# A two-layer graph attention kernel: twelve node tiles of source alphas gathered from a DRAM table, and W1's last third run first

## The chip, the core and the metric

The kernel runs on one core of a Trainium2 chip. The metric is the device time of one execution in microseconds (us). Times are compared as medians of several runs.

A core has five engines with queues of their own that matter here. PE multiplies matrices, and loads its weights beside that (PEld). DVE works on vectors, ACT applies activation functions and copies with a scale, and POOL issues the gathers (DMAs whose rows are picked by a list of indices) and a few other DMAs. SP issues most of the plain DMAs. Each works through its queue in order, and semaphores tie them together.

## The reference

A graph has 3125 nodes with 768 features and 53,125 edges, sorted by destination: 25,000 random pairs in both directions, and a loop at each node. The input is normalised and passed through a relu, and two attention layers follow, with residuals.

```python
def gat_conv(x, edge_index, W, a_src, a_dst, bias, heads, out_ch, concat):
    xl = (x @ W).reshape(n, heads, out_ch)
    alpha_src = einsum('nhc,hc->nh', xl, a_src)
    alpha_dst = einsum('nhc,hc->nh', xl, a_dst)
    e = leaky_relu(alpha_src[src] + alpha_dst[dst], 0.2)
    e = exp(e - segment_max(e, dst)[dst])
    alpha = e / (segment_sum(e, dst)[dst] + 1e-16)
    out = segment_sum(xl[src] * alpha[:, :, None], dst)
    ...
h0 = relu(layernorm(x))
h1 = relu(layer_norm(gat_conv(h0, W1, 4 heads of 256))) + h0 @ Wr1 + br1
h2 = layer_norm(gat_conv(h1, W2, 1 head of 768)) + h1 @ Wr2 + br2
return x + h2
```

So each edge needs, for each of the four heads of layer 1, the alpha of its source node and that of its destination node, and the row of its source node.

## The kernel before, in words

The nodes are cut into 25 tiles (NB) of 128, the last of 53. The edges that end in one node tile are laid out as 17 columns (J) of 128 slots. An alpha of an edge is kept in `al1[slot, column, head, node tile]`. The change lies in layer 1, ahead of its weighted sums, where three stages follow one another.

**First stage: products.** `ring` holds eight tiles of x. A loop over b runs from -2 to 25. In each turn DVE takes the statistics of tile b + 2 (`stats`) and normalises tile b + 1 (`normal`, L814), PE transposes tile b and ACT applies the relu (`flip`, L822), and then two things are interleaved by hand. The first is the product of h0 with W1. W1 is extended by eight columns, the weights folded with a_src1 and a_dst1 (`fold`), so that the product also gives the alphas of each node. It has 1032 columns, cut in three thirds of 344 (`product(b, i)`, L854). The last third (i = 2) holds the alphas. They go into `asad1` and `known` counts the tiles that have them. The finished row goes to `table1` in DRAM, from where layer 1 gathers later. `products` (L875) runs all three thirds of a tile, one tile after another, apart from the first three tiles. W1 is loaded by thirds, too.

The second thing is the side work, the generator `beside` (L945), of which `quota` says how many steps a turn takes: one or two in the first turns, then two, and three from turn 13 on. Its steps, in order: the fold of W1 with a_src1 and a_dst1 (four steps), the list of edges (`edge_list`, L253, with the two matmuls of L315 and L358 that sum the edges by node), the first step of `windows` (L363, which starts a gather of the list), the fold of W2 (`fold_w2`, L882), the rest of `windows` (which gives `idx_s`, the source node of each slot, and tables in DRAM of 16-bit lists), and `own_lookups` (L906). The last compares lists with node numbers to find, by bf16 matmuls, the destination's alpha of each slot. It takes the alphas in groups, as `known` allows. The comparison (`one_hot`) is stored in `hot_d` for layer 2 as an 8-bit float, by a converting DMA of POOL (L931), and ACT counts its ones into `cnt` (L934).

The orders of PE, ACT and DVE in this stage are those of the program. After the loop come the products that are left, six steps of `early` (L993: h0 times Wr1 for twelve tiles, 144 matmuls as written), and what is left of the side work. Each matmul in fp32 is two instructions of the profile.

**Second stage: source lookups** (L1075). The alphas of the sources need a lookup over all nodes. For each of 25 node tiles, a list of 2176 low parts of the source numbers is spread over all partitions and compared with the node number (`one_hot`), 51 matmuls pick for each slot the alphas of the 25 nodes with that low part (`source_values`, L553), DVE multiplies these with a mask of the high part, and one reduction writes `al1[:, :, :, b]` (L567). Between the tiles PE takes four or five steps of `early` (112 in all).

**Third stage: softmax** (`weights`, L598). It transposes `al1` (L581), scans along the lists for the largest alpha and applies the exponential, with 26 more steps of `early` between. Then the weighted sums of layer 1 begin (L758), with gathers of 4 KB rows of `table1` by POOL (L197). The first ten of these are issued as soon as `table1` is whole. The layer 2 that follows isn't touched.

## Time and profile before

| what | value |
|---|---|
| runs shown (three) | median 1917.48 us, from 1916.97 to 1924.33 |
| the profiled execution | 1923.87 us; its span 1922.0 us; mean granted clock 0.96 |
| busy: PE, DVE, ACT, POOL | 1759.3, 1000.4, 443.7, 898.9 us |
| W1 products: first and last start | 11.7 to 302.4 us |
| source lookups: first and last start | 313.0 to 476.0 us |
| first weighted sum of layer 1 | 507.0 us |

The page gives one line per group of instructions: line of the code, engine, operation, what is written from what, shapes, count, then the busy time, the mean duration of one in ns, and the idle time of the engine just ahead, with what ended it. A timeline has one line per instruction or run of like instructions: start and duration in us, then the same names; the bracket has the idle time before it and what ended that. Durations of matmuls overlap, so that PE's rate is read from one start to another. A view of windows gives the busy time of each engine in stretches of the span.

### The profile page before, as it was taken

Reading aid. Unit: us, or ns where it says so; the run is one execution under the profiler, and the core shown is the slowest. Engines: PE = TensorE matmul, PEld = TensorE weight load, DVE = VectorE, ACT = ScalarE, POOL = GpSimd, SP = SyncE. Lnnn points to the kernel's source line nnn. Section 1 sums busy time; section 2 is a strip of 40 time slices with the busy share of each in tenths; the row PEclk is TensorE's granted clock in tenths of the full one; section 3 lists DMA queues with packets and bytes.
Section 4 is the critical chain, followed back from the end, with each engine's and each line's share of the span. In section 5 each row is a group of like instructions: output and inputs, shape, how many; then the busy total and the mean of one; then the engine's idle time right before and its main releaser. Section 6 shows DMA issues by size and latency. Waiting matters only on the chain. (4 is left out here: it accounts for less than half of the span.)

```text
span 1922.0 us, 31113 instructions
## 1 busy us (share of the span) xinstructions
PE 1759.3 (92%) x11411; PEld 957.8 (50%) x11411; DVE 1000.4 (52%) x2641; ACT 443.7 (23%) x1286; POOL 898.9 (47%) x922
## 2 busy tenths in 40 slices
PE   8999998999879999999998998969888898988895
PEld 5666664666446655555554554434333333333331
DVE  7673434888845566466466556312433443344345
ACT  2122331000211212112111211212322332333233
POOL 2000102000365666566566666156566666666662
PEclk9999999999889999999998999889889999989998
DMA  7824538331598999999899999488888998988984
GB/s 236 281 96 144 135 110 295 115 126 64 203 407 314 367 372 348 356 374 385 329 356 378 349 377 333 156 324 313 302 286 324 329 328 325 327 311 310 328 284 157
DMA packets 173673, 540.78 MB, mean 281 GB/s; under 512 B 33086, under 2 KB 58452, under 8 KB 173384
## 3 DMA queue, kind: packets, MB, share of 16 engines
q0 software_dynamic: 100912, 381.05, 55.2%
q1 hardware_dynamic: 68206, 147.26, 21.9%
q10 hardware_dynamic: 4394, 10.39, 1.4%
q8 instruction: 93, 1.52, 0.3%
q14 instruction: 68, 0.56, 0.1%
HBM read 498.62 MB, written 65.62 MB: 294 GB/s over the span
## 5 line engine op out<-in xcount | busy, mean ns | idle before, releaser
L197 POOL DMA_INDIRECT g<-table,idx_s x406 | 405.2, 998 | 411.7 <-DVE m L635 179.2
L201 POOL DMA_INDIRECT g<-table,hi_s x426 | 437.7, 1027 | 291.7 <-issue 88.8
L758 PE MATMUL pa<-g,w 128*32 128x256 f32 x3912 | 275.9, 395 | 32.6 <-issue 23.9
L1377 PE MATMUL pa<-g,w 128*32 128x384 f32 x1956 | 248.8, 510 | 58.9 <-issue 54.4
L182 PE MATMUL pr<-wr,h 128*128 128x384 f32 x768 | 288.0, 516 | 3.8 <-issue 3.8
L182 PE MATMUL p<-w,h1T 128*128 128x384 f32 (+1 forms) x768 | 278.7, 511 | 2.2 <-DVE h1T L1181 1.6
L758 PEld LDWEIGHTS pa<-g,w 128*32 128x32 f32 x3912 | 131.7, 112 | 166.3 <-issue 78.7
L182 PEld LDWEIGHTS pr<-wr,h 128*128 128x128 f32 x768 | 144.8, 200 | 126.2 <-issue 58.2
L182 PEld LDWEIGHTS p<-w,h1T 128*128 128x128 f32 x768 | 145.1, 197 | 123.9 <-issue 32.5
L735 DVE TENSOR_TENSOR w<-oh,al 128x128 f32<-128x128 f32 (+1 forms) x416 | 132.0, 317 | 130.5 <-PE pa L758 75.0
L1377 PEld LDWEIGHTS pa<-g,w 128*32 128x32 f32 x1956 | 63.7, 111 | 221.4 <-issue 208.4
L1341 DVE CUSTOM_DVE_ANT_0 e<-mix,pen 128x640 f32<-128x640 f32 x25 | 20.6, 825 | 290.4 <-remote 132.3
L863 PE MATMUL pm<-w,h0l 128*128 128x344 f32 (+1 forms) x468 | 140.8, 455 | 0.0
L182 PE MATMUL pr<-h0k,wr 128*128 128x256 f32 (+1 forms) x576 | 140.1, 390 | 0.0
L1000 PE MATMUL pm<-h0g,wr 128*128 128x512 f32 x288 | 132.7, 607 | 0.1
L863 PE MATMUL pm<-w,h0g 128*128 128x344 f32 x432 | 131.0, 459 | 0.3 <-ACT h0g L842 0.3
L182 PEld LDWEIGHTS pr<-h0k,wr 128*128 128x128 f32 x576 | 106.2, 190 | 29.5 <-issue 9.0
L931 POOL DMA_DIRECT2D hot_d<-ohd x25 | 13.4, 538 | 219.5 <-DVE own L513 120.6
L734 DVE TENSOR_SCALAR oh<-iota_f,rel_s 128x32 f32<-128x32 f32 (+1 forms) x416 | 113.4, 272 | 0.1
L863 PEld LDWEIGHTS pm<-w,h0l 128*128 128x128 f32 (+1 forms) x468 | 84.8, 185 | 44.1 <-issue 5.7
L863 PEld LDWEIGHTS pm<-w,h0g 128*128 128x128 f32 x432 | 81.9, 193 | 40.8 <-issue 1.7
L1320 ACT ACTIVATE slots<-g 128x32 f32<-128x32 f32 x416 | 65.1, 219 | 117.8 <-DMA g<-table,idx_s 77.7
(288 smaller groups left out, 1666.8 us busy)
## 6 DMA issues: line engine op xcount, KB each, us to landing
s<-slo_d SPq DMA_DIRECT2D x25, 544.0 KB
table<-row SPq DMA_DIRECT2D x24, 512.0 KB
own<-table SPq DMA_DIRECT2D x24, 512.0 KB
h1T_d<-h1T SPq DMA_DIRECT2D x24, 512.0 KB
h<-h1T_d SPq DMA_DIRECT2D x22, 512.0 KB
table<-row SPq DMA_DIRECT2D x24, 392.0 KB
ring<-in_x_dram SPq DMA_DIRECT2D x24, 384.0 KB
xr<-in_x_dram SPq DMA_DIRECT2D x24, 384.0 KB
```

Of the source, the lines that this page charges most:

```text
L182: nc.tensor.matmul(out_, lhsT, rhs, start=start, stop=stop)
L197: nc.gpsimd.indirect_dma_start(out=g, out_offset=None, in_=table[:, :], in_offset=bass.IndirectOffsetOnAxis(ap=idx_s[:, c], axis=0))
L201: nc.gpsimd.indirect_dma_start(out=g, out_offset=None, in_=table[:, :], in_offset=bass.IndirectOffsetOnAxis(ap=idx_k[:, c], axis=0), bound ...
L734: nc.vector.tensor_scalar(oh, iota_f[:, lo:hi], rel_s[:, c:c + 1], None, op0=OP.is_equal)
L735: nc.vector.tensor_tensor(w, oh[:, None, :].to_broadcast([128, heads, hi - lo]), al[:, POS[j], :, b:b + 1].to_broadcast([128, heads, hi - ...
L758: nc.tensor.matmul(pa[p0:p0 + 32, o // f, o % f:o % f + n], w[:, o // cols, :], g[:, o:o + n], start=to not in opened, stop=False, skip_gr ...
L863: nc.tensor.matmul(pm[:r, :C], h0[b][:, k, :], w1[:, k, i * C:(i + 1) * C], start=(k == 0), stop=(k == NK1 - 1))
L931: nc.gpsimd.dma_start(hot_d[b], ohs[b])
L1000: nc.tensor.matmul(pm, wr1[:, k, m * 128:(m + 1) * 128], groups[gi][:, k, :], start=(k == 0), stop=(k == NK1 - 1))
L1320: nc.scalar.activation(slots[b % 2][:, POS[j], :], gs[b, j][:, C2:C2 + 1].to_broadcast([128, 32]), AF.Copy)
L1341: nc.vector.tensor_tensor_reduce(out=e, in0=mix[:, :WIN], in1=pen, scale=1.0, scalar=-BIG, op0=OP.add, op1=OP.max, accum_out=top)
L1377: nc.tensor.matmul(pa[p0:p0 + 32, i, :f], w_, g[:, i * f:(i + 1) * f], start=(i, q) not in opened, stop=False, skip_group_check=True)
```

## The change

- Source alphas of tiles 0 to 11 (`gathered`) are no longer looked up. `asad1`'s source half is written, in four pieces, to a new table in DRAM, `as1_d` (16 bytes per node), and the new generator `alphas` has POOL gather it, one DMA for each column of 128 slots, into `got`; POOL copies each finished tile into its column of `al1`.
- So that the alphas of all nodes are there early, the loop over b runs the last third of W1 for every node tile as soon as it is flipped, with one or two products per turn (`turns`). The first two thirds of tiles 3 to 24 (`rest`), but for five products that are put in turns 9 to 13, come after the loop, and there side work and gathers are interleaved with them.
- The row of a tile is stored in two parts, the last third on its own.
- The side work has a new order (the fold of W2 behind all of `windows`, nine empty steps ahead of its second step) and new quotas: three steps in turns 3 to 7, one in 8 to 13, then two.
- The one-hot of the own lookups is converted to 8 bits by ACT, in the instruction that counts, and SP stores it.
- The second stage runs for tiles 12 to 24 (`looked`), with the same 112 steps of `early` spread over 13 tiles.

```diff
--- before.py
+++ after.py
@@ -138,6 +138,7 @@
     keep_d = dram.tile([H * NB, S + 2], BF16, name="keep_d")
     hot_d = dram.tile([NB, 128, WIN], F8, name="hot_d")
     ball_d = dram.tile([C2], F32, name="ball_d")
+    as1_d = dram.tile([NB * 128, H], F32, name="as1_d")
 
     ident = const.tile([128, 128], F32, name="ident")
     make_identity(nc, ident)
@@ -786,6 +787,7 @@
             ring = mp.tile([128, NK1 * HC // D, D], F32, tag="B", name="ring")
             AHEAD = NK1 * HC // D
             h0, groups, later_in = {}, [], {}
+            gathered, looked = range(12), range(12, NB)
             so = right.enter_context(tc.tile_pool(name="so1", bufs=1, side="right"))
             own = so.tile([128, J, 2 * H, NB], F32, name="own")
             tabs = so.tile([P, 3, H, NB], BF16, name="tabs")
@@ -847,37 +849,51 @@
                             nc.sync.dma_start(h0T_d[i][:, :, :cols_of(i)], later_in[i])
 
                 C = W1C // 3
-                LEAD = 3
                 rows1 = {}
                 known = 0
+                saved = [9, 17, 23, NB]
 
                 def product(b, i):
 
                     nonlocal known
                     r = rows_of(b)
                     if i == 0:
-                        rows1[b] = wp.tile([P, HC], F32, name="row", bufs=LEAD)[:r]
-                    row = rows1[b]
+                        rows1[b] = wp.tile([P, 2 * C], F32, name="row", bufs=3)[:r]
+                    row = wp.tile([P, HC - 2 * C], F32, name="rowa", bufs=3)[:r] if i == 2 else rows1[b]
+                    o = 0 if i == 2 else i * C
                     pm = pm1.tile([128, 512], F32, name="pm", bufs=3)
                     for k in range(NK1):
                         nc.tensor.matmul(pm[:r, :C], h0[b][:, k, :], w1[:, k, i * C:(i + 1) * C],
                                          start=(k == 0), stop=(k == NK1 - 1))
                         if k == NK1 - 1:
                             e = min((i + 1) * C, HC) - i * C
-                            nc.scalar.activation(row[:, i * C:i * C + e], pm[:r, :e], AF.Copy)
+                            nc.scalar.activation(row[:, o:o + e], pm[:r, :e], AF.Copy)
                             if e < C:
                                 nc.scalar.activation(asad1[:r, b, :], pm[:r, e:C], AF.Copy)
                                 known = b + 1
-                                store_rows(nc.sync, table1, b, row)
+                                store_rows(nc.sync, table1[:, 2 * C:], b, row)
+                                if known in saved:
+                                    g0 = ([0] + saved)[saved.index(known)]
+                                    nc.sync.dma_start(
+                                        as1_d.rearrange("(b p) v -> p b v", p=128)[:, g0:known, :],
+                                        asad1[:, g0:known, :H])
+                            elif i == 1:
+                                store_rows(nc.sync, table1[:, :2 * C], b, rows1.pop(b))
                         if k % 3 == 2:
                             yield
 
-                def products():
-                    for b, i in ((0, 0), (1, 0), (0, 1), (2, 0), (1, 1), (2, 1), (0, 2), (1, 2), (2, 2)):
+                ahead_of = [(0, 0), (1, 0), (0, 1), (2, 0), (1, 1), (2, 1)]
+                rest = [(b, i) for b in range(3, NB) for i in range(2)]
+                turns = {1: ahead_of[:2], 2: ahead_of[2:4], 3: ahead_of[4:], 4: [(0, 2), (1, 2)],
+                         5: [(2, 2), (3, 2)], 6: [(4, 2), (5, 2)]}
+                for b in range(7, NB + 1):
+                    turns[b] = [(b - 1, 2)]
+                    if 9 <= b < 14:
+                        turns[b].append(rest.pop(0))
+
+                def products(todo):
+                    for b, i in todo:
                         yield from product(b, i)
-                    for b in range(LEAD, NB):
-                        for i in range(3):
-                            yield from product(b, i)
 
                 def fold_w2():
                     with tc.tile_pool(name="wf", bufs=2, side="right", reuse_waits="tile") as fp:
@@ -906,7 +922,6 @@
                 def own_lookups():
 
                     with tc.tile_pool(name="sd1", bufs=1, side="right", reuse_waits="tile") as sb:
-                        junk = sb.tile([128, WIN], BF16, name="junk")
                         ohs, tabd = {}, {}
                         ds_ = {b: window(sb, b) for b in range(3)}
                         yield
@@ -928,10 +943,11 @@
                         for b in range(NB + 1):
                             if b < NB:
                                 ohs[b] = one_hot(sb, ds_.pop(b), WIN, "ohd")
-                                nc.gpsimd.dma_start(hot_d[b], ohs[b])
                                 if b + 3 < NB:
                                     ds_[b + 3] = window(sb, b + 3)
-                                nc.scalar.activation(junk, ohs[b], AF.Copy, accum_out=cnt[:, b:b + 1])
+                                hot = sb.tile([128, WIN], F8, name="hot", bufs=3)
+                                nc.scalar.activation(hot, ohs[b], AF.Copy, accum_out=cnt[:, b:b + 1], saturate=False)
+                                nc.sync.dma_start(hot_d[b], hot)
                             if b in upto:
                                 while known < min(upto[b] + 1, NB):
                                     yield
@@ -939,8 +955,6 @@
                             if b:
                                 own_values(own, b - 1, own_products(H, pp, ohs.pop(b - 1), tabd[b - 1]))
                             yield
-
-                products_ = products()
 
                 def beside():
 
@@ -952,14 +966,15 @@
                         yield from edge_list(ep, pp)
                     lists = windows(pp)
                     next(lists)
-                    yield
-                    yield from fold_w2()
+                    for _ in range(9):
+                        yield
                     for _ in lists:
                         yield
+                    yield from fold_w2()
                     yield from own_lookups()
 
                 work = beside()
-                quota = {-2: 1, -1: 0, 0: 1, 1: 2, 2: 2}
+                quota = {-2: 1, -1: 0, 0: 1, 1: 2, 2: 2, 3: 3, 4: 3, 5: 3, 6: 3, 7: 3}
                 for b in range(2):
                     fetch(b)
                 for b in range(-2, NB + 1):
@@ -980,12 +995,14 @@
                         flip(b)
                     if b <= 3:
                         stats(b + 2)
+                    todo = products(turns.get(b, ()))
                     for i in range(3):
-                        if b > 0:
-                            next(products_, None)
-                            next(products_, None)
-                        if i < quota.get(b, 2 if b < 13 else 3):
+                        for _ in range(2 if b < 7 else 1 if i < 2 else 9):
+                            next(todo, None)
+                        if i < quota.get(b, 1 if b < 14 else 2):
                             next(work, None)
+                    for _ in todo:
+                        pass
                 wr1 = mp.tile([128, NK1, HC], F32, tag="B", name="wr1")
                 for k in range(NK1):
                     nc.sync.dma_start(wr1[:, k, :], Wr1[k * 128:(k + 1) * 128, :])
@@ -1007,9 +1024,32 @@
                                             nc.sync.dma_start(r1T_d[soon[gi * GB + i]][:, m - 1:m + 1, :], rt[:, i])
                                 yield
 
+                def alphas():
+
+                    ready = []
+                    for b in gathered:
+                        got = so.tile([128, J, H], F32, name="got", bufs=3)
+                        for j in range(J):
+                            nc.gpsimd.indirect_dma_start(
+                                out=got[:, POS[j], :], out_offset=None, in_=as1_d[:, :],
+                                in_offset=bass.IndirectOffsetOnAxis(ap=idx_s[:, b * J + j:b * J + j + 1], axis=0))
+                        ready.append((got, b))
+                        if len(ready) > 1:
+                            t, o = ready.pop(0)
+                            nc.gpsimd.tensor_copy(al1[:, :, :, o], t)
+                        yield
+                    t, o = ready.pop(0)
+                    nc.gpsimd.tensor_copy(al1[:, :, :, o], t)
+
                 fill = early()
                 sum_biases(mp)
-                for _ in products_:
+                asks = alphas()
+                for n, _ in enumerate(products(rest)):
+                    if n % 2:
+                        next(work, None)
+                    if n % 6 == 0:
+                        next(asks, None)
+                for _ in asks:
                     pass
                 for _ in range(6):
                     next(fill)
@@ -1072,8 +1112,8 @@
                     by_chunk(g1, None, NK2, g1_c)
                     by_chunk(be1, None, NK2, be1_c)
                     slots = ends_of_lists()
-                    for b in range(NB):
-                        for _ in range(4 + b % 2):
+                    for n, b in enumerate(looked):
+                        for _ in range((n + 1) * 112 // len(looked) - n * 112 // len(looked)):
                             next(fill, None)
                         t = sb.tile([128, S], I16, name="s", bufs=2)
                         nc.sync.dma_start(t, slo16_d[b * S:(b + 1) * S][None, :].to_broadcast([128, S]))
```

## The prediction

> **What bounds the kernel now.** I read the windows first, then PE's and DVE's instructions in order of time in the first stage, then one node tile of the second stage, then POOL. The profiled execution took 1923.87 us, 1.87 us of it outside the span of 1922.0 us; the median of the runs shown is 1917.48 us. I work out a difference against the profiled execution and take it off the median.
>
> ```profile
> 0.00:50.00 50.00, 40.69 (x146) 27.54 (x147) 37.76 (x162) 10.97 (x30) 11.89 (x29) 1.00 0.73 238
> 100.00:150.00 50.00, 50.00 (x202) 33.72 (x201) 38.91 (x68) 10.42 (x30) 0.00 (x0) 1.00 0.32 102
> 200.00:250.00 50.00, 50.00 (x238) 33.71 (x238) 22.87 (x69) 19.57 (x55) 6.91 (x13) 1.00 0.50 139
> 400.00:450.00 50.00, 50.00 (x491) 32.04 (x489) 42.94 (x57) 4.12 (x6) 0.00 (x0) 1.00 0.36 123
> ```
>
> Columns: stretch and length, then busy time and count of PE, PEld, DVE, ACT, POOL, then clock, DMA share, GB/s. PE has no idle time from 100 us on, in the stage of the products (to 302 us) and in that of the source lookups (to 476 us). DVE is nearly full in the lookups and in the first 150 us, where the lists of edges are made. POOL does nothing in 400 to 450. So the change takes work from PE and DVE where both are full, and gives it to an idle engine.
>
> ```profile
> 399.83 1.77 PE L562 MATMUL pq<-tabs,ohs 128*128 128x100 bf16 x36
> 401.45 4.52 PE L1000 MATMUL pm<-h0g,wr 128*128 128x512 f32 x10
> 405.80 2.45 PE L562 MATMUL pq<-tabs,ohs 128*128 128x100 bf16 x51
> 408.09 3.66 PE L1000 MATMUL pm<-h0g,wr 128*128 128x512 f32 x8
> ...
> 476.00 4.52 PE L1000 MATMUL pm<-h0g,wr 128*128 128x512 f32 x10
> ...
> 480.36 2.02 PE L581 MATMUL pq<-ident,al 128*100 128x128 f32 x17
> ```
>
> A node tile's lookups are 51 matmuls in 408.09 - 405.80 = 2.29 us; ten matmuls of the filling product last 405.80 - 401.45 = 4.35 us, 0.435 each (a written fp32 matmul is two of them). The filling is not removed: it has 112 steps in this loop, before and after. At 480.36 al is transposed for the softmax, 4.36 us behind the last lookups: this is the point that everything later hangs on.
>
> **Removed.** Twelve tiles' lookups are 12 x 2.29 = 27.5 us of PE, and DVE loses twelve times its share. Of the 13 tiles that stay, each has 112 / 13 = 8.62 filling steps: 17.2 x 0.435 + 2.29 = 9.79 us of PE. Their DVE work is four products, a one-hot, a mask and a reduction:
>
> ```profile
> L564 DVE TENSOR_TENSOR scr<-pq,ohh 128x500 f32<-128x500 f32 x75 | 49.9, 677 | 27.6 <-PE pq L562 21.7 <-remote 5.9
> L567 DVE TENSOR_REDUCE al<-scr 128x68 f32<-128x1700 f32 x25 | 48.0, 1920 | 0.1
> L530 DVE TENSOR_SCALAR ohs<-s,node_f 128x2176 bf16<-128x2176 int16 x25 | 19.6, 785 | 2.4 <-DMA s<-slo_d 2.4
> L1082 DVE TENSOR_TENSOR ohh<-iota_f,hi_s 128x425 bf16<-128x425 f32 x25 | 14.9, 596 | 1.1 <-DMA ball_d<-ball_v 1.1
> ```
>
> That is about 5.7 us (the fourth product is shorter), so PE alone bounds the stage: 13 x 9.79 = 127.3 us.
>
> From the last product (its start is the 302.4 of the first row below) to the transposes of al: 12 filling matmuls (5.2), the 13 tiles (127.3), 4.4 behind them: 136.9 us. Before, it was 480.36 - 302.4 = 178 us, 13 us more than the sum of its parts (5.2 + 25 x 6.22 + 4.4 = 165), because own lookups and the first one-hots came late there, behind the last product:
>
> ```profile
> L863 PE MATMUL pm<-w,h0l x468: 452/452/557, 17.5 to 302.4; 128*128 128x344 f32 x144, 128*53 128x344 f32 x12
> ...
> 302.80 0.39 PE L545 MATMUL pd<-tabd,ohd 128*128 128x96 bf16 x5
> 303.02 5.38 PE L1000 MATMUL pm<-h0g,wr 128*128 128x512 f32 x12
> ...
> 313.01 2.37 PE L562 MATMUL pq<-tabs,ohs 128*128 128x100 bf16 x46
> ```
>
> After, own lookups end among the products, and 5.2 us and 8.6 filling steps cover the first one-hot. So if the first stage stays as long as it is, the gain is 178 - 136.9 = 41 us.
>
> **Moved: the order of the first stage.** PE's work there is the same, but no longer spread evenly. Until now each node tile brings three products and one flip:
>
> ```profile
> 62.98 10.57 PE L863 MATMUL pm<-w,h0g 128*128 128x344 f32 x36
> 73.39 0.82 PE L840 MATMUL pt<-ident,ring 128*128 128x128 f32 x6
> 74.05 10.58 PE L863 MATMUL pm<-w,h0l 128*128 128x344 f32 x36
> ```
>
> A product is 10.41 / 3 = 3.47 us, a flip 0.66: PE is busy for 11.1 us per tile, and DVE's steps beside it may wait that long unseen. After, a tile brings two products (7.6 us of PE) up to tile 6 and in 9 to 13, and one (4.1 us) otherwise, while DVE keeps its order: normalising, then steps of the side work, more of them per tile than before. A flip waits for a normalisation that DVE does behind the side work of the tile before the last. I laid PE's, DVE's and ACT's instructions one behind another in program order, with the durations of the rows and these waits. For the kernel before this ends the products at 302.3 us (trace: 302.4). For the change, it gives four places where PE runs dry.
>
> (1) The edge totals. DVE reaches them unhindered, and PE has six products by then, not ten:
>
> ```profile
> 29.72 0.68 DVE L820 TENSOR_SCALAR ring<-ring,bn_mv,bn_rs 128x768 f32<-128x768 f32 x1
> ...
> 47.55 0.27 DVE L304 TENSOR_TENSOR cnt<-cnt,part 125x101 f32<-125x101 f32 x1
> ...
> 50.05 0.57 DVE L306 TENSOR_REDUCE cnt<-own 125x1 f32<-125x425 f32 x1
> ...
> 52.47 0.25 DVE L318 COPY tot<-pe 1x103 f32<-1x103 f32 x1 [0.43 <-PE pe L315]
> ...
> 58.06 0.20 DVE L355 CAST two<-at 1x100 f32<-1x100 int32 x1
> ```
>
> Flip 3 waits until 30.4; with two products PE is done at 38.0. The matmul of the totals stands next in PE's queue, now in tile 3's turn: it needs the reduction, which DVE begins at 47.7 and ends at about 49.8. PE stands for 11.7 us, with flip 4 and all products queued behind it. The second matmul (L358) needs DVE's 5.7 us from 52.47 to 58.2 and a normalisation ahead of them, beside one product: another 3.3 us. With 2.7 at flip 3, and 4.5 us of such waits that are already there, 13 us more than before.
>
> (2) The windows of the list. They start when the gathered list lands, some 2.5 us behind this:
>
> ```profile
> 70.99 1.08 POOL L368 DMA_INDIRECT w_in<-views_d,view  x1 [21.21 <-DMA views_d<-pk_d]
> ...
> 95.50 0.58 DVE L388 TENSOR_SCALAR w_a<-w_in,base 100x704 int32<-100x704 int32 x1
> ...
> 123.43 0.83 DVE L409 CUSTOM_DVE_ANT_0 w_in<-w_in,w_a 100x1280 uint16<-100x1280 uint16 x1
> ```
>
> Between 95.50 and 124.2 DVE takes 27 us for them. After, they begin at about 73.5, with three normalisations between, and tiles 7 and 8 have only 4.1 us of PE work each: waits of 2.6, 1.1 and 2.4 us at flips 9 to 11, 6 us in all.
>
> (3) The fold of W2, moved to tiles 18 to 20.
>
> ```profile
> L900 DVE SCALAR_TENSOR_TENSOR w2t<-w2k,ab 128x768 f32<-128x768 f32 x16 | 15.3, 958 | 12.2 <-DMA w2k<-in_L_gnn_W_dram 11.9
> ...
> 185.54 0.39 DVE L530 TENSOR_SCALAR ohd<-near,node_f 128x640 bf16<-128x640 int16 x1 [14.44 <-DMA near<-rel_d]
> ```
>
> 16 us of DVE, the loads of W2 ahead (12 us of waiting before, when a large copy ran beside them), and then the windows of the own lookups (14 us of waiting, SP being held up by row stores). I take 5 us for each wait, nearer to a quiet queue than to these rows, since the row stores now come every 4 us; 3 and 12 are the ends. PE has 4.1 us per tile here: 16 us of waits (12 to 28).
>
> (4) After the long stop PE is slow for a while, as at its start:
>
> ```profile
> 11.88 5.81 PE L863 MATMUL pm<-w,h0g 128*128 128x344 f32 x12
> 17.54 3.63 PE L863 MATMUL pm<-w,h0l 128*128 128x344 f32 x12
> ```
>
> 2.2 us at the first of these; I add 2. In all 13 + 6 + 16 + 2 = 37 us: the products end at 339.4 instead of 302.4, and the loop, which 39 products and the remaining own lookups follow (139.5 us), at 200.
>
> **Added on POOL.** 12 x 17 = 204 gathers of 128 rows of 16 bytes. The trace has none so small; its nearest are these:
>
> ```profile
> 307.20 1.01 POOL L197 DMA_INDIRECT g<-table,idx_s  x1 [2.21 <-PE pm L1000]
> ...
> 309.79 1.32 POOL L197 DMA_INDIRECT g<-table,idx_s  x1 [0.30 <-issue]
> 311.42 0.94 POOL L197 DMA_INDIRECT g<-table,idx_s  x1 [0.30 <-issue]
> 312.66 1.04 POOL L197 DMA_INDIRECT g<-table,idx_s  x1 [0.30 <-issue]
> ...
> 319.09 0.94 POOL L197 DMA_INDIRECT g<-table,idx_s  x1 [0.30 <-issue]
> L701 POOL DMA_INDIRECT ao<-alo_d,at_last x5 | 4.8, 964 | 6.1 <-DMA alo_d<-scr 4.9 <-issue 0.9 <-DVE oh L734 0.3
> ```
>
> Start to start the commonest is 1.24 us (311.42 to 312.66); nine steps from 307.20 to 319.09 make 1.32. L701's rows are 800 bytes, not 4096, and cost the same, so the count of rows sets it. I take 1.28: 261 us. With 3 us for the last store of alphas to land and twelve copies at 0.5 us (no row; between 0.1 and 1), al is whole at 200 + 3 + 261 + 6 = 470, and wanted at 339.4 + 136.9 = 476.3. It is hidden, by 6 us. Because both chains hang on the loop's end, this reserve stays whatever (1) to (4) are. The ten table gathers at 307 us queue behind on POOL: 13 us more, to 483, wanted 22 us behind 480 or so. The stores now come as two per tile, the one-hots go out on SP, and no engine waits for them soon; ACT writes the one-hot in place of a scratch tile: nothing.
>
> **The sum.** al is transposed at 476.3 instead of 480.4: 4 us earlier, and all behind it is as it was. 1917.5 - 4.1 = 1913 us.
>
> **Rivals.** A: the first stage hardly grows, because the loads come sooner than I bound them, or the queues stand otherwise than in program order. For it: the number of gathered tiles fits POOL's time. Against: in the trace these instructions do stand in program order. With waits of 10 to 20 us the gain is 21 to 31 us: 1886 to 1896.
>
> B, the slower side: POOL ends last. It decides from 1.31 us a gather on; each 0.1 more costs 20 us. At 1.42 (between the mean of 1.32 and the single 1.63 from 309.79 to 311.42) al is whole at 499, 23 us behind need: 1936. For it: the gathers run beside DVE work for 261 us; against: those ten did too. [...]
>
> C: POOL's and DVE's writes to al, which interleave by column, are taken for a conflict. Then DVE's first reduction waits for POOL's last copy at 470, and the 13 tiles follow: over 100 us slower, beyond 2020. No row speaks for it.
>
> **Chances.** What differs by less than 0.5%, 9.6 us, is about what a measurement here can't tell from none. The forecast's own case (waits of 30 to 45 us, POOL hidden or nearly) has 0.50: 1905 to 1928, of which 0.11 faster, 0.33 within, 0.06 slower. A 0.23, all faster. B 0.20: 0.04 within, 0.16 slower. C 0.04, and 0.03 for a first stage longer still, slower. Together 0.34, 0.37, 0.29. The range goes from 1892, in the middle of A, to 1941, B at 1.45: left out are half of A, C and the end of B.
>
> **What would show it.** PE idle at the totals' matmul (L315) some 12 us; waits of flips for normalisation near the fold of W2; the last product at 330 to 350; 204 gathers 1.24 to 1.32 apart that begin near 200 and end near 465; no wait of PE for POOL's copies at the transposes. I am wrong if the last product comes before 320, if the gathers are over 1.35 apart, or if the first reduction into al waits for POOL.

## The result, and the profile after

| what | before | after |
|---|---|---|
| runs in the same job (a set of kernels run together) | median 1917.22 us (1915.88 to 1924.33, 4 runs) | median 2191.02 us (2181.98 to 2200.22, 4 runs) |
| the profiled execution, its span | 1923.87 us, 1922.0 us | 2181.98 us, 2180.1 us |
| last product of W1 (start) | 302.4 us | 605.2 us |
| first and last source lookup | 313.0 to 476.0 us | 617.7 to 739.7 us |
| transposes of al | 480.4 us | 744.1 us |
| first weighted sum of layer 1 | 507.0 us | 771.3 us |

The ratio is 1.1415, with a 95% interval from 1.1374 to 1.1457: the change makes the kernel 14% slower. At the transposes of al the changed kernel is 263.7 us behind the kernel before; the span is 258.1 us longer. So all of the loss has come by the end of the second stage. The windows show where (columns as in the prediction: stretch, busy PE, PEld, DVE, ACT, POOL with counts, granted clock, DMA share, GB/s):

```profile
250.00:300.00 50.00, 6.60 (x17) 4.00 (x17) 0.88 (x2) 1.17 (x3) 38.20 (x43) 0.56 0.13 22
300.00:350.00 50.00, 6.70 (x17) 4.02 (x17) 0.98 (x2) 1.17 (x3) 38.51 (x43) 0.53 0.10 17
450.00:500.00 50.00, 5.62 (x17) 3.49 (x17) 0.94 (x2) 1.49 (x4) 28.39 (x32) 0.57 0.07 7
500.00:550.00 50.00, 41.92 (x163) 27.58 (x163) 10.51 (x55) 9.59 (x24) 0.00 (x0) 0.88 0.17 59
```

From 250 to 500 us PE is busy for 5 to 7 us in 50, DVE for one or two, ACT for about one, and the DMA engines are nearly idle, at a share of 0.10. Only POOL works, at the gathers:

```profile
L1033 POOL DMA_INDIRECT got<-as_d,idx_s x204 | 193.5, 949 | 223.7 <-DMA as_d<-asad 149.6 <-issue 72.9 <-DMA got<-as_d,idx_s 0.6
```

```profile
221.56 0.98 POOL L1033 DMA_INDIRECT got<-as_d,idx_s  x1 [149.57 <-DMA as_d<-asad]
222.85 0.95 POOL L1033 DMA_INDIRECT got<-as_d,idx_s  x1 [0.31 <-issue]
```

```profile
491.49 0.94 POOL L1033 DMA_INDIRECT got<-as_d,idx_s  x1 [1.16 <-issue]
...
494.87 0.31 POOL L1042 COPY al<-got 128x68 f32<-128x68 f32 x1 [1.87 <-DMA got<-as_d,idx_s]
```

The 204 gathers run from 221.56 to 492.4, mostly 1.25 us apart, and the last copy into al is at 494.87. POOL does what the prediction said. The other engines wait for one another, beside them:

```profile
263.09 0.46 ACT L870 ACTIVATE row<-pm 128x344 f32<-128x344 f32 x1 [24.18 <-remote]
...
277.09 0.58 DVE L552 TENSOR_REDUCE own<-pd 128x136 f32<-128x408 f32 x1 [33.41 <-remote]
...
277.73 0.56 PE L546 MATMUL pd<-tabd,ohd 128*128 128x96 bf16 x5 [30.08 <-issue]
...
278.08 6.24 PE L866 MATMUL pm<-w,h0l 128*128 128x344 f32 x12
...
357.59 0.46 ACT L870 ACTIVATE row<-pm 128x344 f32<-128x344 f32 x1 [46.43 <-remote]
```

ACT copies a product's row at 263.09, after 24.18 us of idling; DVE reduces an own lookup at 277.09, after 33.41 us. Both read what PE writes (the same copy, at 218.90, waited for PE's L866 by name; "remote" in the bracket names no engine). PE has waited 30.08 us at its next own lookup for nothing that the profile names ("issue"); it starts as soon as DVE's reduction ends, and a turn later the same wait is put down to that reduction. The following copies come 46.9, 47.6, 47.6 and 47.6 us after one another: in each such turn PE gets through twelve matmuls of a product and five of a lookup, which take 3.75 us otherwise; that is one matmul in 2.8 us. The recorded times of the twelve (278.08 to 284.3) look almost normal, but the copy that waits for the last of them comes at 357.59, counting copies and products back from 513.89, the copy of the product that starts at 508.43: what is late is what the others see of PE. About 16 us behind the last gather it is over, and from 513 on a product takes 3.75 us again, with its lookup.

The kernel before has the same thing on a small scale, in rows that the prediction didn't quote. Its gathers of 4 KB rows run back to back from 307.20 to 321, and this is PE in its lookups from 313.01 on:

```profile
315.92 0.29 PE L562 MATMUL pq<-tabs,ohs 128*128 128x100 bf16 x3 [0.54 <-issue]
316.63 0.20 PE L562 MATMUL pq<-tabs,ohs 128*128 128x100 bf16 x1 [0.42 <-issue]
317.35 0.22 PE L562 MATMUL pq<-tabs,ohs 128*128 128x100 bf16 x1 [0.52 <-issue]
```

From the seventh gather on (315.37), one to three matmuls come every 0.7 us, each time after a wait for nothing. The prediction says that PE has no idle time in the lookups; the view that it took its windows from has one more row:

```profile
300.00:350.00 50.00, 42.36 (x320) 23.73 (x319) 31.20 (x69) 3.97 (x8) 11.55 (x12) 0.93 0.68 244
```

Of the 7.6 us without PE, 5 are a wait for DVE at 336, and some 2 are these. In the weighted sums of both layers, too, gathers come in bursts 1.25 to 1.3 us apart, and PE's waits have the same name:

```profile
L758 PE MATMUL pa<-g,w 128*32 128x256 f32 x3912 | 275.9, 395 | 32.6 <-issue 23.9 <-DVE w L735 4.0 <-DMA g<-table,hi_s 2.9
L1377 PE MATMUL pa<-g,w 128*32 128x384 f32 x1956 | 248.8, 510 | 58.9 <-issue 54.4 <-DVE v L1403 4.3
```

These are 23.9 and 54.4 us of waiting put down to "issue".

### The profile page after: what moved, and what is told of

The parts are those of the page before. It is cut to its first block, busy times and chain, and to the rows that moved or that the text cites. A ratio compares the mean times of both kernels' runs of the same rounds, so it can differ in the third digit from the quotient of the medians.

```text
span 2180.1 us, 30067 instructions
## 1 busy us (share of the span) xinstructions
PE 1736.4 (80%) x10799; PEld 932.8 (43%) x10799; DVE 938.6 (43%) x2557; ACT 445.2 (20%) x1286; POOL 1082.5 (50%) x1113
## 5 line engine op out<-in xcount | busy, mean ns | idle before, releaser
L202 POOL DMA_INDIRECT g<-table,hi_s x426 | 432.2, 1015 | 282.4 <-PE pa L759 106.1
L1033 POOL DMA_INDIRECT got<-as_d,idx_s x204 | 193.5, 949 | 223.7 <-DMA as_d<-asad 149.6
L759 PE MATMUL pa<-g,w 128*32 128x256 f32 x3912 | 270.1, 392 | 34.2 <-issue 24.7
L546 PE MATMUL pd<-tabd,ohd 128*128 128x96 bf16 x125 | 10.7, 224 | 240.9 <-issue 154.5
L759 PEld LDWEIGHTS pa<-g,w 128*32 128x32 f32 x3912 | 124.6, 111 | 170.1 <-issue 79.4
L1417 PEld LDWEIGHTS pa<-g,w 128*32 128x32 f32 x1956 | 64.6, 111 | 221.0 <-issue 194.9
L866 PE MATMUL pm<-w,h0l 128*128 128x344 f32 (+1 forms) x468 | 154.9, 485 | 0.0
L866 PE MATMUL pm<-w,h0g 128*128 128x344 f32 x432 | 139.8, 478 | 0.0
L552 DVE TENSOR_REDUCE own<-pd 128x136 f32<-128x408 f32 x25 | 14.6, 582 | 270.7 <-remote 212.5
L1017 PE MATMUL pm<-h0g,wr 128*128 128x512 f32 x288 | 127.7, 596 | 0.1
L546 PEld LDWEIGHTS <-ohd 128*128 128x128 bf16 x125 | 8.8, 105 | 250.3 <-issue 246.0
```

Of the source, the lines that this page charges most:

```text
L202: nc.gpsimd.indirect_dma_start(out=g, out_offset=None, in_=table[:, :], in_offset=bass.IndirectOffsetOnAxis(ap=idx_k[:, c], axis=0), bound ...
L759: nc.tensor.matmul(pa[p0:p0 + 32, o // f, o % f:o % f + n], w[:, o // cols, :], g[:, o:o + n], start=to not in opened, stop=False, skip_gr ...
L866: nc.tensor.matmul(pm[:r, :C], h0[b][:, k, :], w1[:, k, i * C:(i + 1) * C], start=(k == 0), stop=(k == NK1 - 1))
L1017: nc.tensor.matmul(pm, wr1[:, k, m * 128:(m + 1) * 128], groups[gi][:, k, :], start=(k == 0), stop=(k == NK1 - 1))
L1033: nc.gpsimd.indirect_dma_start(out=got[:, POS[j], :], out_offset=None, in_=as1_d[:, :], in_offset=bass.IndirectOffsetOnAxis(ap=idx_s[:, b ...
L1417: nc.tensor.matmul(pa[p0:p0 + 32, i, :f], w_, g[:, i * f:(i + 1) * f], start=(i, q) not in opened, stop=False, skip_group_check=True)
```

## The experiments

The theory that I formed from the two traces (T1): gathers that follow one another without a pause hold up PE, and SP with it, while they run. The first rival (T2): the new order of products and own lookups makes the stop by itself. All changes below are against the kernel named.

**The order alone.** No tile is gathered, all 25 are looked up.

```diff
-            gathered, looked = range(12), range(12, NB)
+            gathered, looked = range(0), range(NB)
```

> The changed kernel without its gathers: all 25 tiles are looked up as before, in the new order of the first stage. T1 (the gathers hold up the other engines while they run): no long stop of PE is left, and the time is that of the new order alone, by the prediction's numbers last product at 339 us, 165 us to the transposes of al, 24 us more than before: 1941 us, up to 1960 if the first stage runs some 15 us longer than that. T2 (the new order of products and own lookups itself makes the stop): the stop of some 250 us stays and the time is about 2200 us.

1974.76 us; ratio to the kernel before 1.0289 (1.0255 to 1.0322). No long stop:

```profile
L866 PE MATMUL pm<-w,h0l x468: 452/453/782, 16.3 to 361.0; 128*128 128x344 f32 x144, 128*53 128x344 f32 x12
```

```profile
236.54 0.56 PE L546 MATMUL pd<-tabd,ohd 128*128 128x96 bf16 x5 [7.48 <-DVE own L552]
```

The last product starts at 361.0, al is transposed at 535.8, 55.4 us behind the kernel before: T2 falls for the stop. The order costs more than the 24 us that the prediction's numbers give, though; its parts are below.

**The gathers elsewhere.** The order-only kernel, and 17 gathers behind the lookups of each of tiles 0 to 11, started by a copy of that tile's al on POOL; nobody reads what they bring.

```diff
+                        if n < 12:
+                            nc.gpsimd.tensor_copy(gate, al1[:, :, :, b])
+                            for j in range(J):
+                                nc.gpsimd.indirect_dma_start(out=got[:, POS[j], :], ...as1_d, idx_s...)
```

> As the order-only kernel, with 204 gathers of 16-byte rows whose result nobody reads, 17 behind each of the first twelve tiles' lookups in the second stage. Each group waits for the alphas of its tile, so that POOL starts some 20 us later than the first lookup. T1 (gathers of 16-byte rows, one behind another, hold up PE whatever it does): about 200 to 260 us more than the order-only kernel, and PE's lookups stand at one matmul per 1.4 us or slower. T2 (only the products together with own lookups suffer): no difference from the order-only kernel over 10 us.

2214.41 us, 240 us more than the order-only kernel. Lookups beside gathers, and the lookups of one tile after a pause of the gathers:

```profile
397.56 0.24 PE L563 MATMUL pq<-tabs,ohs 128*128 128x100 bf16 x1 [2.57 <-issue]
400.35 0.24 PE L563 MATMUL pq<-tabs,ohs 128*128 128x100 bf16 x1 [2.55 <-issue]
...
417.36 2.44 PE L563 MATMUL pq<-tabs,ohs 128*128 128x100 bf16 x51
```

One bf16 matmul in 2.8 us instead of 51 in 2.4 us. So it isn't the products, nor fp32, nor who reads the result.

**Half of the gathers.** The changed kernel with `gathered, looked = range(6), range(6, NB)`.

> The changed kernel with 6 tiles gathered and 19 looked up: 102 gathers. T1 (PE stands as long as gathers follow one another): the stop lasts about 130 us instead of 260, and the time is about 2190 - 130 + 6 x 2.3 = 2070 us. T2 (a fixed event, such as a conflict on the first copy, makes the stop): the time stays above 2150 us.

2063.55 us, 127 us less than the changed kernel, although six more tiles are looked up for 14 us. So 102 gathers fewer save about 141 us, 1.4 us each. The stop lasts as long as the gathers do.

**Wider rows.** The table's rows padded to 256 bytes and gathered whole.

```diff
-    as1_d = dram.tile([NB * 128, H], F32, name="as1_d")
+    as1_d = dram.tile([NB * 128, 64], F32, name="as1_d")
-                        got = so.tile([128, J, H], F32, name="got", bufs=3)
+                        got = so.tile([128, J, 64], F32, name="got", bufs=2)
```

> The changed kernel with rows of the alpha table padded to 256 bytes (zeros, written once early), gathered whole; only the first 16 bytes of each are used. T1a (the stop comes from the small size of the rows): PE keeps its pace while the gathers run, and the time falls to 1920 to 1980 us. T1b (any gathers in an unbroken row do it): the stop stays, about 2190 us.

2184.95 us, and 17 matmuls in 50 us as before: not the small rows (T1b).

**Pauses.** The kernel before, and POOL clears a scratch tile ahead of each of the extra gathers.

```diff
+                            for pause in (1400, 900, 600, 300, 0):
+                                for _ in ask(J, 128):
+                                    nc.gpsimd.memset(slack[:, :pause], 0.0)
```

> The kernel before, with 5 groups of 17 gathers of 16-byte rows beside the source lookups, whose results nobody reads. Ahead of each gather POOL clears 1400, 900, 600, 300 or no elements per partition (0.204 us for 128 and 0.10 for one element in the trace of before make about 0.8 ns an element: starts 2.5, 2.1, 1.8, 1.6 and 1.25 us apart); between the groups it clears for about 7 us. T1 (something that gathers share with the other engines is filled faster than it drains, and only a full one holds them up): PE keeps 6.2 us a tile in the slow groups and slows down only in the fast ones; where it begins gives the rate. T2 (each gather costs PE a fixed time): the tiles are longer in all groups, by about 1.2 us a gather, so 15 us or more in each group.

The program put the gathers without a pause among the longer clearings between the groups, so that four paces were measured: starts about 2.5, 1.98, 1.72 and 1.475 us apart. PE, from the end of the third group into the fourth (464.70 to 488):

```profile
458.03 2.45 PE L563 MATMUL pq<-tabs,ohs 128*128 128x100 bf16 x51
...
470.45 2.52 PE L563 MATMUL pq<-tabs,ohs 128*128 128x100 bf16 x51
...
477.89 0.31 PE L563 MATMUL pq<-tabs,ohs 128*128 128x100 bf16 x3 [0.33 <-issue]
478.62 0.34 PE L563 MATMUL pq<-tabs,ohs 128*128 128x100 bf16 x4 [0.42 <-issue]
```

In the first three groups, 51 gathers, a tile's lookups take 2.45 us, apart from the first, which take 4.02 behind a stop, and one that DVE splits. In the fourth it is as fast for about nine gathers, and then comes in pieces 0.7 us apart. So a gather doesn't cost PE a fixed time (T2): 51 of them 1.72 us apart and more left the lookups at 2.45 us, and at 1.475 a wait built up. The time, 1950.87 us, says nothing on this: the ten table gathers came late behind the probe.

**Fewer rows.** The kernel before with 34 gathers of 32 rows, 34 of 64 and 34 of 128, without pauses. Six long clearings were to make breaks of some 12 us between the groups; the program put five or six gathers of the next group among them, 2.9 us apart.

> The kernel before, with 34 gathers of 32 rows, 34 of 64, 34 of 128, one behind another, each group followed by about 10 us without any, then 17 plain transfers by POOL of 128 rows of 16 bytes; nobody reads the results. T1 (the rows of a gather, so its descriptors, are what costs): groups of 32 and 64 rows leave PE at 6.2 us a tile, the group of 128 rows holds it up from about the seventh gather on. T2 (the gather as an instruction is what costs): PE is held up in all three groups alike. If the plain transfers hold PE up as well, gathers are not special.

2038.33 us. All three groups hold PE up (T2: the gather as an instruction). Those of fewer rows do it more, and they also follow faster: late in the first two groups PE does one matmul in 2.8 us, late in the third one in some 1.9, beside gathers 1.165, 1.20 and 1.25 us apart. The end of the first group, whose last gather is issued at 357.16:

```profile
354.05 0.24 PE L563 MATMUL pq<-tabs,ohs 128*128 128x100 bf16 x1 [2.56 <-issue]
...
368.07 0.24 PE L563 MATMUL pq<-tabs,ohs 128*128 128x100 bf16 x1 [1.17 <-issue]
...
370.89 0.41 PE L563 MATMUL pq<-tabs,ohs 128*128 128x100 bf16 x3 [0.85 <-issue]
...
376.88 2.52 PE L563 MATMUL pq<-tabs,ohs 128*128 128x100 bf16 x46
```

PE goes on in single steps of up to 2.8 us until 371, 13 us behind that gather; in the second group it lasts some 10 us, in the third 5. That looks like a backlog that has to drain, beside gathers 2.9 us apart in the first two, and that is shorter where the group's gathers were further apart. The plain transfers in this kernel came 2.3 us apart, between clearings, and tell nothing.

**The pauses in the changed kernel.** First for six tiles, with 900 elements cleared ahead of each gather:

> The kernel with 6 tiles gathered (2063.6 us in one run), and a clearing of 900 elements per partition ahead of each gather, so that they start about 2.1 us apart: 102 gathers from 222 to about 440 us, still ahead of need. T1 (only gathers faster than some rate hold the others up): the stop is gone, and the time is that of the order-only kernel less six tiles' lookups, 1974.8 - 14 = 1961 us. T2 (a fixed cost for each gather): about 2060 us as without the pauses, or more.

2063.44 us. But here POOL ran the clearings while it waited for the table, and then the gathers 1.25 us apart as without them, so that this is the six-tile kernel a second time. With POOL's instructions held in program order and 600 elements:

```diff
-    ...tc.manual_schedule(engines={PE}):
+    ...tc.manual_schedule(engines={PE, POOL}):
+                            nc.gpsimd.memset(slack, 0.0)
                             nc.gpsimd.indirect_dma_start(out=got[:, POS[j], :], ...
```

> Six tiles gathered, with a clearing of 600 elements ahead of each gather, and POOL's instructions kept in program order, so that gathers start 1.72 us apart (the slowest-spaced group that was still cheap in the paced probe was 1.72). 102 gathers take 175 us, from about 225 to 400, ahead of need. T1 (gathers are free for the others when they start at least 1.7 us apart): 1974.8 - 6 x 2.29 = 1961 us, and PE full from 250 us on. T2 (the stop belongs to the products): about 2060 us.

1970.23 us in one run: T1, 93 us faster than without pauses, though 9 us over the forecast. The same for all twelve tiles:

> The changed kernel (12 tiles gathered) with the same pauses: 204 gathers 1.72 us apart take 351 us, so al is whole at about 225 + 351 + 6 = 580 us, some 70 us behind PE (order-only kernel: transposes at 535.8, less 12 x 2.29). T1: PE keeps its pace until it waits for POOL's last copies at the transposes: 1974.8 + (580 - 536) + about 10 for table gathers that come later = 2025 to 2035 us, 160 us faster than the changed kernel although POOL takes longer. T2 (stop belongs to the products, or a fixed cost for each gather): 2190 us or more.

2035.57 us in one run, 155 us faster than the changed kernel, although POOL takes longer:

```profile
250.00:300.00 50.00, 50.00 (x215) 32.92 (x214) 19.80 (x71) 12.57 (x32) 45.46 (x59) 1.00 0.32 87
300.00:350.00 50.00, 50.00 (x175) 32.84 (x174) 0.00 (x0) 6.68 (x15) 45.28 (x60) 1.00 0.18 53
...
500.00:550.00 50.00, 0.00 (x0) 0.00 (x0) 3.27 (x2) 0.00 (x0) 45.49 (x57) 0.52 0.06 7
```

PE is full beside gathers 1.72 us apart, ends its products at 362 and its lookups at 495.3, and then waits for POOL's last copies: al is transposed at 586.6. At 1.72 us 204 gathers are too many to be hidden, and at 1.25 they hold PE up.

**A part of the order undone.** The order-only kernel with the fold of W2 where it was, ahead of the rest of the list's windows.

> The order-only kernel (1974.8 us) with the fold of W2 back in its old place, between the two parts of the list's windows. T1 (the prediction's step 3: the fold costs PE 16 us of waits at tiles 18 to 21, where it has one product per tile, and then some 5 us of slow clock): 1950 to 1960 us. T2 (these waits come from the queues, whatever stands there): within 5 us of 1974.8.

1999.31 us, ratio 1.0436 (1.0384 to 1.0489): 25 us slower than the order-only kernel, so both expectations were wrong.

```profile
91.42 1.54 PE L842 MATMUL pt<-ident,ring 128*128 128x128 f32 x6 [13.44 <-DVE ring L822]
...
109.37 1.51 PE L842 MATMUL pt<-ident,ring 128*128 128x128 f32 x6 [11.45 <-DVE ring L822]
...
132.47 1.51 PE L842 MATMUL pt<-ident,ring 128*128 128x128 f32 x6 [17.05 <-DVE ring L822]
```

The waits at flips 20 and 21 (17.8 us in the order-only kernel) are gone, but flips 7 to 9 now wait 42 us for a normalisation, behind the fold and the windows together. DVE's side work has too little PE work beside it in either place, and the place that the change gives it is the better one.

**The kernel before with paced gathers.** Its own order of the first stage; five tiles gathered 1.73 us apart beside the lookups of the other twenty.

> The kernel before, with its own order of the first stage; the alphas are written to the DRAM table when all are known, and five tiles are gathered 1.72 us apart beside the lookups of the other 20, over which the 112 steps of filling are spread. T1: 85 gathers end at about 303 + 3 + 146 = 452 us, POOL is not late, and the time is that of before less 5 x 2.29 = 11 us: 1906 to 1912 us. T2 (even paced gathers cost PE something, or the ten table gathers that now come behind them are missed): 1915 to 1930 us.

1921.4 us, ratio 0.9991 (0.9963 to 1.0020): no difference. The gain is there in PE's work, and POOL is late:

```profile
317.83 1.04 POOL L1082 DMA_INDIRECT got<-as_d,idx_s  x1 [8.17 <-DMA as_d<-asad]
...
474.83 0.31 POOL L1088 COPY al<-got 128x68 f32<-128x68 f32 x1 [1.98 <-issue]
```

Gathers begin at 317.83, after POOL waited 8.17 us for the table's store to land, and the last copy is at 474.83; PE's last lookups end at 458.8 and the transposes wait until 475.2. The ten table gathers come behind that.

**Pauses in the layers.** The kernel before, 400 bf16 elements cleared ahead of every gather of table rows in both layers.

> The kernel before, with a clearing of 400 bf16 elements ahead of each gather of table rows in both layers, and POOL in program order: these gathers of 4 and 3 KB come in bursts 1.29 us apart in the kernel before, beside which the trace has PE waiting for nothing it shows (24 us in layer 1, 47 in layer 2). T1 (these waits are the same stop, and they cost time): 20 to 60 us faster. T2 (they are hidden, as the DMA engines are full there, and POOL at 406 gathers in 720 us has little room): the same or up to 40 us slower.

1972.08 us, ratio 1.0284 (1.0234 to 1.0334).

```profile
L760 PE MATMUL pa<-g,w 128*32 128x256 f32 x3912 | 276.6, 399 | 41.8 <-DMA g<-table,hi_s 30.5 <-DVE w L737 4.0 <-DVE z L694 3.3
...
L1379 PE MATMUL pa<-g,w 128*32 128x384 f32 x1956 | 192.1, 515 | 3.5 <-DVE v L1405 3.5
```

The waits for "issue" are no longer among the largest in either layer (23.9 and 54.4 us before), as they should be if they were the same hold-up. But layer 1, with its DMA engines nearly full (a share of 0.94 to 0.98 from 500 to 1200 us), lasts as long as before (721 us from the first weighted sum to the last), with POOL busy for 88 us in 100, and in layer 2 POOL, busy for 89 us in 100, is late: its first weighted sum comes 2 us sooner than before, its last 46 us later.

**A job without the hold-up.** In the job of the next four kernels the kernel before took 1804.14 us (1798.67 to 1807.28) instead of 1917 to 1922, with nothing changed in it. The chip was not the difference: the kernels with pauses in program order had run on the same one, and there the kernel before took 1922.19. First, four tiles, with the table stored by POOL:

> As the kernel with five paced tiles in the old order, which was as fast as before because its gathers began at 317.8 us and ended at 471.6, behind need: now four tiles, and the table of alphas is stored by POOL itself, so that no load of SP queues behind that store. 68 gathers 1.73 us apart from about 311 end at 429. T1 (nothing else stood against it): 4 x 2.29 = 9 us less than before, 1908 to 1915 us. T2 (the ten table gathers, which then come 110 us later and among lookups, cost as much): 1918 to 1925 us.

1795.31 us against 1804.14; ratio 0.9958 (0.9943 to 0.9974), so 8 us of the 9. One of its eight executions took 9405.75 us, for which nothing on record gives a cause; the ratio leaves it out.

**Three rates.** The kernel before and three groups of 34 gathers beside the lookups, planned 1.60, 1.475 and 1.36 us apart.

> The kernel before with three groups of 34 gathers of 16-byte rows beside the lookups, whose results nobody reads; the pauses clear 450, 300 and 150 elements: by the paced probe (300: 1.475 us apart; 600: 1.72) starts 1.60, 1.475 and 1.36 us apart, with about 12 us without gathers between groups. T1 (each gather occupies something shared for about 1.4 to 1.6 us): no waits of PE at 1.60; waits that begin late in the group at 1.475, and early and long at 1.36, going on for some us behind the last gather. T2 (a steady share, with no store that fills): PE is slower from the first gather of a group on, and at once fast behind the last.

1851.67 us, with the table gathers late, from 519 us on. PE has no such wait in the first two groups, nor, at 1.35 us a gather, beside the first 20 of the third group's 34, after which PE has other waits.

**Plain transfers.** The kernel before, and on POOL 17 clearings and 51 plain transfers beside the lookups.

> The kernel before with, on POOL beside the lookups, 17 clearings of 2048 elements (31 us), then 51 plain transfers of 128 rows of 16 bytes from the alpha table, back to back. T1 (the gathers' indexed issue is what the others stand behind): PE keeps 6.2 us a tile beside the clearings and beside the plain transfers. T2 (any transfer that POOL issues does it): PE is held up from about the seventh transfer on. If the clearings hold it up, it is POOL's work as such.

1805.98 us, with PE at full pace, 2.45 us a tile's lookups, beside clearings and plain transfers. It is the kernel before apart from these. Its first table gathers now come beside lookups, from 460.58 on:

```profile
461.92 0.97 POOL L198 DMA_INDIRECT g<-table,idx_s  x1 [0.30 <-issue]
463.19 0.94 POOL L198 DMA_INDIRECT g<-table,idx_s  x1 [0.31 <-issue]
...
473.14 0.94 POOL L198 DMA_INDIRECT g<-table,idx_s  x1 [0.30 <-issue]
```

```profile
465.41 2.45 PE L563 MATMUL pq<-tabs,ohs 128*128 128x100 bf16 x51
...
471.19 2.45 PE L563 MATMUL pq<-tabs,ohs 128*128 128x100 bf16 x51
```

```profile
L759 PE MATMUL pa<-g,w 128*32 128x256 f32 x3912 | 257.6, 392 | 21.1 <-DMA g<-table,hi_s 9.5 <-DVE w L736 7.6 <-DVE z L693 2.4
```

Eleven gathers 1.25 us apart, and the lookups keep 2.45 us; the waits for "issue" in the layers are not there either. So in this job the hold-up was missing, and the kernel before took some 115 us less. This kernel and the one above therefore tell nothing of paces or of plain transfers where it is present.

**A short pause in the layers.** The kernel before, 16 elements cleared ahead of every gather of table rows.

> The kernel before with a clearing of only 16 elements ahead of each gather of table rows in both layers, POOL in program order: gathers of a burst are then some 1.5 us apart instead of 1.29. The longer pause removed PE's waits for nothing shown, but filled POOL (90%) and made layer 2 50 us longer. T1 (some pause between is a net gain): 5 to 20 us faster than before. T2 (the waits are hidden behind the full DMA engines): the same or up to 15 us slower.

1816.0 us, ratio 1.0068 (1.0050 to 1.0086): in this job without the hold-up, the pauses cost 12 us and gained nothing.

To see whether the change gains what it was priced at without the hold-up, the changed kernel and its order alone ran once more.

> The changed kernel once more, unchanged. In the last four runs the kernel before itself took 1804 us instead of 1917 to 1922, and the trace had none of PE's waits for nothing shown beside the bursts of table gathers. T1 (the hold-up is a condition that these runs were free of): where the kernel before takes about 1804, the changed kernel has no stop and takes the order-only kernel's time less 12 x 2.29 = 27 us, about 1830. Where the kernel before takes about 1920, it takes about 2190 again. T2 (the hold-up belongs to unbroken gathers everywhere, and the last runs escaped it by their pauses): about 270 us over the kernel before in either case.

> The order-only kernel once more, beside the changed kernel. T1: 54 us over the kernel before in either case (1858 where that takes 1804), since its loss is DVE's side work and PE's slow clock in the first stage, not gathers. T2 (part of its loss was the hold-up too): less than 40 us over the kernel before where that takes 1804.

In this job the kernel before took 1920.89 us again, and the two 2190.0 (ratio 1.1383, 1.1343 to 1.1423) and 1970.63 us (1.0248, 1.0216 to 1.0280): the loss repeats, and the question stays open.

## Why the prediction was wrong

The step that failed is the one that let 204 gathers run beside the other engines at no cost: "It is hidden, by 6 us", with "those ten did too" for the only test of it. POOL's own time was nearly right: 1.25 us a gather against 1.28, and 12 copies of 0.32 us, though not for the reason given ("the count of rows sets it"): a quarter of the rows takes 1.165 instead of 1.25 us. What was never priced is what unbroken gathers do to the others. In 250 us of them PE did what takes it some 20 us. The last product starts at 605.2 where 339.4 was forecast. Beside the order-only kernel it is 605.2 - 361.0 = 244 us later; the other 22 us of the error are the order's.

Point by point:

- **Edge totals (1)**: PE stood 11.55 us at L316 (forecast 11.7), 1.57 at L359 (3.3) and 2.42 at flip 3 (2.7); less the 2.9 us of such waits before, 12.7 us against 13.
- **Windows (2)**: 4.63 and 0.80 us at flips 9 and 11, 5.4 against 6.
- **Fold of W2 (3)**: 11.38 and 5.18 us, 16.6 against 16.
- **Slow clock (4)**: here a size was off. Not 2 us in all, but 1.5 to 3 at each of five stops, some 10 us in all, since PE starts again slowly each time. The last two, where the granted clock was 0.59 from 172.7 to 178.4 us and 0.73 from 185.2 to 189.8, and 1.00 from 190.5:

```profile
171.36 1.51 PE L842 MATMUL pt<-ident,ring 128*128 128x128 f32 x6 [11.38 <-DVE ring L822]
172.66 5.98 PE L866 MATMUL pm<-w,h0l 128*128 128x344 f32 x12
183.83 1.51 PE L842 MATMUL pt<-ident,ring 128*128 128x128 f32 x6 [5.18 <-DVE ring L822]
185.13 4.88 PE L866 MATMUL pm<-w,h0g 128*128 128x344 f32 x12
189.85 0.82 PE L842 MATMUL pt<-ident,ring 128*128 128x128 f32 x6
```

  A flip takes 1.51 us after a stop and 0.82 otherwise, a product 4.9 to 6.0 instead of 3.63. Ahead of flip 3 PE stood only 2.42 us, and the product behind it (31.07) still took 5.11 us, at a granted clock of 0.71 from 30.2 to 36. The prediction's own sum had these stops in it.
- **After the loop**: in the order-only kernel its last product ends at 210 instead of 200, and then 151 us go by instead of 139.5, mostly because an own lookup waits 7.48 us for DVE at 236.54, and PE starts again slowly behind it (six matmuls of a product take 3.77 us there, twelve took 3.70 ahead of it), with POOL idle. At the same place in the changed kernel (235.12) DVE itself waited 10.14 us for a list that SP loads. So the order alone puts the last product at 361.0, where 339.4 was forecast.
- **Start of the gathers**: 221.56 instead of 203: the loop's last product ends at 210.8 instead of 200, and 11 instead of 3 us go by for the last store of alphas, which SP issues only at 217.77.
- **Second stage**: from the last product to the transposes 744.1 - 605.2 = 138.9 us, forecast 136.9. The twelve tiles do save what was said.
- **Rivals**: none of the three came. A was wrong about the first stage. B expected POOL's end to decide, which it doesn't. C could not show in the changed kernel, where POOL's last copy (494.87) is over before the first lookup (617.7); with paced gathers of all twelve tiles, the lookups, which DVE's reductions into al follow, run from 374.4 to 495.3 us without a wait of PE, though POOL's last copy holds the transposes until 586.6. In these runs PE waited 30.08 us and more at a time beside gathers, and POOL was not delayed: its gathers stayed 1.25 us apart.
- **The signs that I gave**: of the three for being wrong none came, as the last product was later than 320, the gathers were 1.25 us apart and the first reduction did not wait; none would have shown this. Of those for being right, the last product at 330 to 350 failed (605.2), but without a cause; the windows of the first 50 us beside gathers name it.

How sure is what? Shown: the hold-up follows the rate of gathers (it is there in six kernels without pauses, and not beside lookups and products in four with them); gathers of 16 or 256 bytes a row, and of 32, 64 or 128 rows, all do it; it is there with products, own lookups, source lookups and weighted sums; in the jobs that have it, pauses that put the starts 1.72 us apart remove it, 1.475 doesn't quite. Most of these kernels ran once; where their times are compared, the differences are 90 us and more. Only argued: that something which gathers share with PE and SP takes 1.4 to 1.6 us for each, and that a backlog of about eight is taken without harm. Open: what that is, whether plain transfers do it too, why one job was free of it, and what the change would be worth there. The record has a span and a granted clock for every execution, so each seems to have been profiled; whether the hold-up is there without that, no run shows. By the sum of the measured parts (54 us for the order, less about 27 for the lookups) it would still lose, but no run shows it.

## What to carry to other kernels

Before you move work to an idle engine, look in the trace for the longest stretch in which it already does such work without a break, and read the others' waits there, above all waits for nothing that the profile names: eleven gathers in a row were there, and three lines of PE beside them were the warning. A cost per instruction that is right for the engine itself says nothing of what a run of 204 does to its neighbours. And price each stop of PE with its slow restart, 1.5 to 3 us each here.

## What the runs showed of the hardware

- In every job but one, gathers issued by POOL 1.165 to 1.25 us apart slowed PE down, to one matmul in 2.8 us at the worst, from the seventh to tenth gather on, with 32 to 128 rows of 16 or 256 bytes or of 4 KB, and for 3 to 16 us behind the last one. SP's issues are stretched too, though not always: in the changed kernel four loads of one list take 1.77 to 1.81 us from 212.25 to 220, 4.90 to 6.30 us in the five sets from 239.95 to 316, and 1.74 to 2.48 in the sets at 325.70, 420.09 and 467.76. DVE and ACT wait for PE, but their own instructions are not stretched: beside the gathers ACT's three from 357.59 on take 0.46, 0.73 and 0.19 us, and 0.44, 0.74 and 0.19 at 215, and DVE's reduction of an own lookup takes 0.58 us there as in the kernel before.
- The same kernel took 1804 us in one job and 1917 to 1922 in the others, at a granted clock of 0.97 and 0.96. In the free job's kernel with plain transfers, which is otherwise the kernel before, the weighted sums took 681 us instead of 721 in layer 1 and 527 instead of 602 in layer 2 (first start to last), which is all of the difference. In layer 2 the waits put down to "issue" (54.4 us) went with it. In layer 1 they need not be the cause: the kernel with 400 elements cleared in the layers was without them and still took 721 us, with POOL busy for 88 us in 100 instead of 62.
